# Moving the third sweep's last layer norm into both attention arms, with three carried tiles, and the last layer's pair products ahead of a weighing

## The chip, the cores and the metric

The kernel runs on one core of a Trainium2 chip as a single program. The metric is the device time in microseconds (us), as the median of several runs. A core has five engines, each with its own stream of instructions: PE (TensorE: matrix products and transposes; PEld is its weight load), DVE (VectorE), ACT (ScalarE), POOL (GpSimd) and SP (SyncE), which here issues most of the DMA transfers. The engines wait for each other through semaphores. SBUF is the memory that they compute from, PSUM holds PE's results in banks.

## The reference

Four graph layers act on x (4096 nodes by 64 features) with one dense 4096x4096 matrix `adj` of 64 MB, some 98% of it zero, symmetric in its pattern but not in its values. Each layer ends with a residual add and a layer norm.

```python
x = layernorm(x + cheb(x, adj, W0))        # K = 4: terms x, Lx, 2L(Lx)-x, ...; sum of terms @ W[k]
x = layernorm(x + attention_gru(x, adj, adj, ...))
x = layernorm(x + decay(x, adj, W2, b2))
x = layernorm(x + hyperbolic(x, adj, W3, b3))

# layer 1: A = adj without its diagonal d
node = concat([(A > 0) @ h, (A < 0) @ h]);  edge_out = gru_cell(node, h, ...)
hw = h @ W;  e_plus, e_minus = leaky_relu(concat of (A > 0) @ hw and (A < 0) @ hw, times a)
att = softmax(where(A > 0, e_plus, where(A < 0, e_minus, -9e15)), axis=1)
node_out = gru_cell((att * A) @ hw, h, ...)
out = d * edge_out + d * node_out

# layer 2: mask = adj != 0; rank = cumsum(mask, axis=1); k = min(deg, 100)
w = mask * 0.5 ** (k - pos);  out = w @ (x @ W2) + b2     # the last nonzeros of a row weigh most

# layer 3: logmap on the Poincare ball for every pair (i, j), weighted by adj / deg
out = expmap(0, (sum_j w_ij * logmap_xi(xj)) @ W3 + b3)
```

The data are never negative, but a negative entry of `adj` is allowed: the kernel counts negative row minima in the first sweep and chooses between two versions ("arms") of the attention at run time.

## The kernel before

`adj` is handled in tiles of 512 by 512 floats (1 MB): eight groups of 512 rows (`g`, NG = 8) by eight chunks of columns (`c`, NCH = 8), 64 tiles for one pass. A group is four blocks of 128 nodes (GB = 4). Features lie both as `nat_a` (nodes on partitions, 65 columns: 64 features and a one) and as `tr_a` (features on partitions), `sp_two` and `sp_lo` are its parts in narrower types for the attention's products.

**Chebyshev, 0 to 566 us.** A first sweep loads the 64 raw tiles, transposes them on PE and stores them as `adj_t`; a second and a third sweep read tiles of `adj_t` or keep raw ones in SBUF, in a rotating set of five 1 MB slots from the pools `staying` and `going`, handed out by `row_tile`. The third sweep (loop from L692) goes through the groups in the order 7, 0, 6, 1, 5, 2, 4, 3 (`last_row` is 3 in the changed code). When a group's products are done, steps from a list `due` follow: `third_weighed` (L655) weighs the sum with the last Chebyshev matrix, `after_third` (L659) transposes four blocks (L663), adds the residual on DVE (L665, "y"), runs the layer norm, centres `nat_a` (L301) and splits it into narrower types, and `turned_third` (L671) transposes the result back into `tr_a` (`to_columns`, L212). Ahead of the last group's steps, two tiles of attention's first row are loaded into slots (`with_at`) and one mask `adj > 0` is made of the first of them (`positives`, L447).

**Attention, to 865 us.** L1049 reads the flag from memory into a register of each engine, L1051 opens `If` (signed arm, both signs) and `Else` (unsigned arm). The code of the two arms lies one after the other in every engine's stream, so in the unsigned case each engine jumps over the signed arm at its start. Both arms come from `attention(signed, ...)`. It goes through 64 tiles; for each: a product of the mask with `sp_two` (L980, "wide"), one with `sp_lo` (L988, "narrow"), and one of the tile itself (after a step on DVE at L963) with `nat_a` (L997). The masks run two tiles ahead, and each is stored by a POOL DMA to `mask_t` (L724). In the last group, `load2` (L735 to L738) brings the masks of the decay's first chunk back from `mask_t` into eight SBUF tiles, `first_masks`. A group's tail (gates of two GRU cells, norm; `group_end`, L779 to L919) is cut into steps that run beside the next group's tiles; the end of it, `decay_parts`, prepares the next layer, its last operations being four POOL DMAs for each group. The arm ends with copies of `last_p` and `last_a` (L1040 to L1043).

**Decay, to 1067 us.** A tile's mask is counted from the end of the row by a product (L1192, `cnt_ps`), ACT or DVE makes the weight of it (L1197, L1199, `wt`), and PE gathers (L1150, L1162, `acc_ps`). Its sums are copied on DVE (L1215), weighed by PE (L1114, `wd`), and normed in steps. The steps of the last groups ("seam steps") are left over for the last layer.

**Last layer, from 1067 us.** For each group a "right" operand is made (L1283 to L1287); for each tile PE forms pair products `v_ps` (L1327), ACT squares them (L1336), DVE takes one off (L1353, `w`), ACT and DVE form the pair's factor through `rt` (L1545), `f` (L1530) and `at_d` (L1533), and PE gathers (L1387, L1392). Twelve small constants for it are made on DVE just ahead. One seam step, a weighing, is popped before the first rights and products.

Order: a tile scheduler puts the instructions of each engine into an order and gives each a slot in its pool; SP's DMA issues keep program order. An engine executes its own stream in order, so an instruction that waits holds those behind it.

Of the kernel before, what the change touches and what calls it, by code (L numbers as in the profile page):

```python
# [60 lines left out]
def gnn4_kernel(  # L61
# [25 lines left out]
    GB = 4  # L87
# [14 lines left out]

    front = ctx.enter_context(ExitStack())
    front_p = front.enter_context(tc.tile_pool(name="front", bufs=1, side="right"))

    staying_p = front.enter_context(tc.tile_pool(name="staying", bufs=2, side="right"))
    going = ctx.enter_context(ExitStack())
    going_p = going.enter_context(tc.tile_pool(name="going", bufs=3, side="right"))
    places = []

    def row_tile(name):
        places.append(name)
        pool = staying_p if len(places) % 5 in (1, 2) else going_p
        return pool.tile([P, GB, CB * P], F32, name=name, tag="raw")
# [63 lines left out]
    negatives = keep.tile([1, 1], mybir.dt.int32, name="negatives")  # L178
# [26 lines left out]
    def gblocks(g):  # L205
        return slice(g * GB, (g + 1) * GB)
# [238 lines left out]
    def positives(pool, at):  # L445
        pos = pool.tile([P, CB, GW], MASK, name="pos")
        in_order(nc.vector.tensor_scalar(pos, at, 0.0, None, ALU.is_gt, saturate=False))  # L447
        return pos

# [6 lines left out]
    with tc.tile_pool(name="acc", bufs=1) as acc_p, tc.tile_pool(name="win", bufs=1) as win_p, tc.tile_pool(  # L456
# [41 lines left out]

        def mine(g):
            return slice(g % 2 * F, g % 2 * F + F)  # L500
# [61 lines left out]

        loads, weight_steps = attention_weights(win_p, ps_p)
# [61 lines left out]
        for step in steps0:  # L625
            step()

# [6 lines left out]
        nc.vector.tensor_copy(negatives, low_ps)  # L634
# [20 lines left out]
        def third_weighed(g, ps):  # L655
            o, y_t = weigh(g, [(out_of(ps, "t_h"), cheb[:, 3, :])])
            nc.vector.tensor_tensor(y_t, o, y_t, ALU.add)

        def after_third(g):  # L659
            gs = gblocks(g)  # L660
            o = new_post()
            for b in range(GB):
                nc.tensor.transpose(o[:, b, :], acc_t[mine(g), g // 2, cols(b)], ident[mine(g), mine(g)])  # L663
            y = sm.tile([P, GB, F], F32, name="y0", tag="y")
            nc.vector.tensor_tensor(y, o, nat_a[:, gs, 0:F], ALU.add)  # L665
            layernorm(nat_a[:, gs, 0:F], y)
            centre(g)
            split(g, nat_a[:, gs, 0:F], F - 1, sp_hi, sp_mid, sp_lo)
# [23 lines left out]
        for m, g in enumerate(sum(([NG - 1 - i, i] for i in range(NG // 2)), [])):  # L692
            ps = ps_a.tile([P, GW], F32, name="pass3", tag=("h_ps", "w_ps")[m % 2])
            for c in reversed(range(g + 1)):
                at = load0(g, c)
                for k in range(CB):
                    halves(ps, 2, at[:, k, :], c * CB + k, c == g and k < 2, c == 0 and k >= CB - 2)
                later.flush()
                while due and due[0][0] <= n:
                    due.pop(0)[2]()  # L700
                n += 1
            due += [
                (n, m, lambda g=g, ps=ps: third_weighed(g, ps)), (n + 1, m, lambda g=g: after_third(g)),
                (n + 5, m, lambda g=g: turned_third(g)),
            ]
            due.sort(key=lambda d: d[:2])

        with_at = [load1(staying_p, NG - 1, c, "raw") for c in range(2)]
        with_pos = [positives(front_p, with_at[0])]
        for work in due:  # L710
            work[2]()

    going.close()
    three = ctx.enter_context(tc.tile_pool(name="three", bufs=1))

# [30 lines left out]
    first_masks = [late.tile([P, CB, GW], MASK, name=f"first_mask{n}") for n in range(2 * QG)]  # L746
# [6 lines left out]
    def group_end(g, Q, nb, tl, sums, a_t, wq, by_ln=False):  # L753
# [160 lines left out]
        def decay_parts(ps_p):  # L914

            split(g, nat_b[:, gblocks(g), :], F, sup_two[:, :, 0:F], sup_two[:, :, F : 2 * F], sup_lo)
            for there, here in ((over_two, sup_two), (over_lo, sup_lo)):
                for q in range(2):
                    nc.gpsimd.dma_start(  # L919
                        there[(1 - q) * HP : (2 - q) * HP, gblocks(g), :], here[q * HP : (q + 1) * HP, gblocks(g), :]  # L920
                    )
            nc.vector.tensor_tensor(
                nat_b[:, gblocks(g), :], nat_b[:, gblocks(g), :], bd.unsqueeze(1).to_broadcast([P, GB, F]), ALU.add
            )
# [13 lines left out]
        ] + norm, [[nothing]], [[decay_parts]]  # L938
# [5 lines left out]
    def attention(signed, cols_p, sg, tl, ps_a, ps_p):  # L944
# [68 lines left out]
        steps = []  # L1013
        for n, (g, c) in enumerate(order):
            if n + lead < len(order):
                ahead.append(masks(*order[n + lead]))
# [32 lines left out]
    any_negative = nc.values_load(negatives, min_val=0, max_val=P)  # L1049
    for signed in (True, False):  # L1050
        with tc.If(any_negative > 0) if signed else cmp.Else() as block:  # L1051
# [9 lines left out]

    nat_c = ctx.enter_context(tc.tile_pool(name="nat3", bufs=1, side="right")).tile([P, NB, F], F32, name="nat_c")
# [31 lines left out]
    def turn_prepared(ps_p, g):  # L1094
        to_columns(ps_p, tr_a[0 : F + 2, gcols(g)], left.pop(g), F + 2, nc.vector.tensor_copy)
        to_columns(ps_p, tr_o[0:2, gcols(g)], sides[:, gblocks(g), :], 2, nc.vector.tensor_copy)

# [39 lines left out]
    with tc.tile_pool(name="mask2", bufs=3) as mk_p, tc.tile_pool(name="wt2", bufs=3) as wt_p, tc.tile_pool(  # L1137
# [37 lines left out]
        for turn, groups in enumerate(turns_of):  # L1175
            cnt = [ps_c.tile([P, GW], F32, name=f"cnt_ps{a}") for a in range(2)]
            acc = [ps_a.tile([P, GW], F32, name=f"acc_ps{q}") for q in range(QG)]
            if turn == 0:
# [49 lines left out]
    middle.close()  # L1228

# [13 lines left out]
    with tc.tile_pool(name="o3", bufs=1) as op, tc.tile_pool(name="cols3", bufs=3) as cols_p, tc.tile_pool(  # L1243
# [4 lines left out]
        name="ps_p3", bufs=2, space=PSUM  # L1248
    ) as ps_p, tc.tile_pool(name="ps_a3", bufs=2, space=PSUM) as ps_a:
# [3 lines left out]

        to_right = op.tile([P, F + 2], F32, name="to_right")
        to_other = op.tile([P, 2], BF16, name="to_other")

        spread = op.tile([P, F + 1], F32, name="spread")
        spread_w = op.tile([P, F], F32, name="spread_w")
        wh_x = op.tile([P, F], F32, name="wh_x")
# [6 lines left out]

        nc.vector.memset(to_right, 0.0)
        nc.vector.tensor_scalar_mul(to_right[0:F, 0:F], ident[0:F, 0:F], -4.0)
        nc.vector.tensor_scalar_mul(to_right[F : F + 2, F : F + 1], ident[F : F + 2, F + 1 : F + 2], 2.0)
        nc.vector.tensor_scalar_mul(to_right[F : F + 2, F + 1 : F + 2], ident[F : F + 2, F : F + 1], 2.0)  # L1270
        nc.vector.memset(to_other, 0.0)
        nc.vector.tensor_scalar_mul(to_other[0:2, 0:1], ident[0:2, 1:2], OPPOSITE)
        nc.vector.tensor_scalar_mul(to_other[0:2, 1:2], ident[0:2, 0:1], OPPOSITE)
        nc.vector.memset(wh_x, 0.0)
        nc.vector.tensor_copy(wh_x[0:F, :], wh)
        nc.vector.tensor_copy(spread[:, 0 : F - 1], pair[:, 0 : F - 1])
        nc.vector.tensor_scalar(spread[:, F - 1 : F], pair[:, F - 1 : F], -1.0, None, ALU.add)
        nc.vector.tensor_copy(spread[:, F : F + 1], pair[:, F - 1 : F])
# [220 lines left out]
        if seam:  # L1499
            seam.pop(0)(ps_p)  # L1500
# [109 lines left out]
```

## Time and profile before

| what | value |
|---|---|
| runs of the kernel | 1541.69, 1551.27, 1553.98 us; median 1551.27 |
| profiled execution: time | 1546.41 us |
| profiled execution: span of the trace | 1544.3 us, 19446 instructions |
| PE busy | 1410.2 us (91%), 7054 instructions |
| DVE busy | 1066.9 us (69%), 2123 |
| ACT busy | 761.4 us (49%), 1265 |
| POOL busy | 123.8 us (8%), 194 |
| granted PE clock, mean | 0.977 |
| DMA | 385 MB, mean 250 GB/s |
| chain that ended last, by engine | PE 32%, DVE 18%, ACT 6%, issue 2%, DMA 2% |

Busy time is that of the whole span; the stages differ in what limits them, so a share says little about one of them. "Issue" in a chain is time in which an engine waited for nothing that the trace shows. In a line of the timeline the columns are: start (us), length (us), engine, line of the kernel and operation, output and inputs, shapes and types, and in brackets the idle time ahead of it on its engine with what ended it. An x4 or x16 joins so many like instructions. The engine names with a q stand for an engine's sequencer, where branches and register loads run.

### The profile page before, as it was taken

The page shows a single profiled execution, that of the slowest core. Times are in us where ns is not written, and L with a number is a line of the kernel's source. Part 1 is how long each engine was busy: PE and PEld are TensorE (multiplying, and loading weights), DVE is VectorE, ACT ScalarE, POOL GpSimd, SP SyncE. Part 2 cuts the span into 40 slices and gives each one's busy share as a digit, 9 for nine tenths or more (in the row PEclk, how much of TensorE's full clock was granted, in tenths as well). Part 3 has the DMA queues.
Part 4 walks back from the last instruction along what each step waited for, and adds up shares of the span by engine and source line. Part 5 has one row for each costly group of instructions (what it writes and reads, how often), then busy time and mean ns, then how long its engine had stood idle before and what let it go on. Part 6 is the DMA issues. An engine that isn't in the chain of part 4 may idle for free.

```text
span 1544.3 us, 19446 instructions
## 1 busy us (share of the span) xinstructions
PE 1410.2 (91%) x7054; PEld 644.7 (42%) x7054; DVE 1066.9 (69%) x2123; ACT 761.4 (49%) x1265; POOL 123.8 (8%) x194
## 2 busy tenths in 40 slices
PE   5999999999999969889899999998888999899995
PEld 4555655554443323334343333333334444344343
DVE  5899989883000663667666422556999999999997
ACT  3544434441000110222222476654877999899995
POOL 3011000000000001222222200000000000000000
PEclk9999999999999998999999999999999999999997
DMA  9999999996787987888888655553224453445430
GB/s 295 412 404 411 411 410 397 382 358 242 245 287 261 389 342 271 280 309 305 296 309 296 207 177 183 164 165 131 88 109 164 162 195 136 167 156 193 149 113 11
DMA packets 103359, 385.38 MB, mean 250 GB/s; under 512 B 16340, under 2 KB 17368, under 8 KB 71256
## 3 DMA queue, kind: packets, MB, share of 16 engines
q1 hardware_dynamic: 84256, 296.78, 53.9%
q0 software_dynamic: 15616, 85.73, 13.6%
q10 hardware_dynamic: 3384, 1.56, 0.4%
q8 instruction: 57, 0.93, 0.2%
q14 instruction: 46, 0.38, 0.1%
HBM read 297.26 MB, written 85.20 MB: 248 GB/s over the span
## 4 chain that ended last, share of the span: by engine, by line
PE 32%; DVE 18%; ACT 6%; issue 2%; DMA 2%; SPq 0%; ACTq 0%; DVEq 0%
PE v_ps L1327 5%; PE a_ps L997 4%; PE sums_ps L1387 4%; PE cnt_ps L1192 4%; PE acc_ps L1150 4%; DVE rt L1545 3%; DVE at_m L1373 3%; PE p_ps L980 2%; DVE f L1530 2%; DVE at_d L1533 2%; ACT wt L1197 2%; PE post L779 1%; DMA at<-adj_t 1%; PE p_ps L988 1%; DVE w L1353 1%
## 5 line engine op out<-in xcount | busy, mean ns | idle before, releaser
L592 ACT COPY at<-tp 128x512 f32<-128x512 f32 x256 | 132.5, 598 | 137.2 <-issue 96.0
L1327 PE MATMUL v_ps<-rv,tr_a 128*128 128x512 f32 (+1 forms) x288 | 141.5, 616 | 31.7 <-DVE rt L1545 30.3
L1197 ACT ACTIVATE wt<-cnt_ps 128x512 uint16<-128x512 f32 x208 | 115.4, 594 | 72.1 <-PE cnt_ps L1192 70.3
L585 PE MATMUL tp<-ident,raw 128*128 128x128 f32 x1024 | 133.4, 284 | 16.2 <-DMA raw<-in_adj_dram 12.0
L618 DVE TENSOR_REDUCE dpart<-raw 128x4 f32<-128x2048 f32 x64 | 145.4, 2272 | 0.4 <-DMA raw<-in_adj_dram 0.3
L620 DVE TENSOR_REDUCE lows<-raw 128x1 f32<-128x2048 f32 x64 | 145.4, 2271 | 0.0
L1387 PE MATMUL sums_ps<-at_d,nat_c 128*64 128x512 f32 x288 | 139.8, 606 | 1.4 <-DVE at_d L1533 1.0
L585 PEld LDWEIGHTS tp<-ident,raw 128*128 128x128 f32 x1024 | 116.6, 145 | 55.3 <-issue 34.1
L997 PE MATMUL a_ps<-at,nat_a 128*64 128x512 f32 x512 | 126.9, 624 | 2.9 <-DVE at L963 2.9
L447 DVE TENSOR_SCALAR pos<-at 128x2048 fp8e4<-128x2048 f32 x72 | 87.1, 1224 | 58.1 <-DMA at<-adj_t 49.3
L1392 PE MATMUL sums_ps<-at_m,nat_c 128*64 128x512 f32 x224 | 108.6, 607 | 0.0
L492 PE MATMUL w_ps<-at,cheb_n 128*128 128x512 f32 x224 | 101.1, 595 | 0.0
L492 PE MATMUL pass<-at,cheb_n 128*128 128x512 f32 x224 | 99.9, 604 | 0.7 <-DVE cheb_n L643 0.7
L1556 ACT ACTIVATE rt<-rt,one_col 128x1024 f32<-128x1024 f32 x72 | 78.7, 1095 | 22.5 <-DVE rt L1545 22.0
L1327 PEld LDWEIGHTS v_ps<-rv,tr_a 128*128 128x128 f32 x288 | 52.8, 199 | 82.7 <-DVE rt L1545 39.5
L1545 DVE SCALAR_TENSOR_TENSOR rt<-v_ps,rt 128x1024 f32<-128x1024 f32 x72 | 83.2, 1156 | 3.8 <-ACT rt L1521 3.6
L1192 PE MATMUL cnt_ps<-m,follow 128*64 128x512 fp8e4 x480 | 81.1, 391 | 4.7 <-ACT wt L1197 2.3
L1533 DVE TENSOR_TENSOR at_d<-at_d,f 128x1024 f32<-128x1024 f32 x72 | 83.2, 1156 | 0.1
L1530 DVE SCALAR_TENSOR_TENSOR f<-rt,w 128x1024 f32<-128x1024 f32 x72 | 82.9, 1158 | 0.5 <-ACT rt L1556 0.4
L1373 DVE TENSOR_TENSOR at_m<-post,at_m 128x512 f32<-128x512 f32 x112 | 75.3, 683 | 9.3 <-PE post L1371 8.6
L1336 ACT ACTIVATE w<-v_ps,one_col 128x1024 f32<-128x1024 f32 x72 | 75.7, 1053 | 11.3 <-PE v_ps L1327 10.9
L1547 ACT ACTIVATE w<-w,half_shift 128x1024 f32<-128x1024 f32 x72 | 78.7, 1094 | 0.9
(365 smaller groups left out, 2267.3 us busy)
## 6 DMA issues: line engine op xcount, KB each, us to landing
at<-adj_t SPq DMA_DIRECT2D x122, 1024.0 KB, 6.1
raw<-in_adj_dram SPq DMA_DIRECT2D x64, 1024.0 KB, 13.7
adj_t<-at POOLq DMA_DIRECT2D x64, 1024.0 KB, 8.2
at_d<-adj_t SPq DMA_DIRECT2D x36, 1024.0 KB, 4.8
at_m<-adj_t SPq DMA_DIRECT2D x28, 1024.0 KB, 6.8
mask_t<-pos POOLq DMA_DIRECT2D x64, 256.0 KB, 5.9
m<-mask_t SPq DMA_DIRECT2D x120, 128.0 KB, 2.8
m<-mask_t SPq DMA_DIRECT2D x60, 256.0 KB, 3.9
```

The source lines that it names most:

```text
L492: in_order(nc.tensor.matmul(ps, lhsT=cheb_n[:, jb, k : k + 2, :], rhs=rhs, start=first, stop=last))
L585: in_order(nc.tensor.transpose(tp[:, cols(b)], raw[:, b, cols(k)], ident))
L592: nc.scalar.copy(at[:, k, :], tp)
L618: in_order(nc.vector.tensor_reduce(dpart[:, g, c, :], raw, AX.X, ALU.add))
L620: in_order(nc.vector.tensor_reduce(lows[:, n : n + 1], raw.rearrange("p b j -> p (b j)"), AX.X, ALU.min))
L997: in_order(nc.tensor.matmul(ps[q * F : (q + 1) * F, :], lhsT=nat_a[:, c * CB + k, 0:F], rhs=parts[q if signed else 0][:, k, :], start=(c = ...
L1192: in_order(nc.tensor.matmul(cnt[a][r * HP : (r + 1) * HP, :], lhsT=follow, rhs=chunks[c][odd][2 * a + r][:, k, :], start=(h == 2 * NB - 1) ...
L1197: in_order(nc.scalar.activation(wt[odd][a], cnt[a], AF.Relu, scale=-128.0))
L1327: nc.tensor.matmul(vs[n][:, k, cs], lhsT=tr_a[:, cols(jb)], rhs=rights[i][0][:, cs], start=True, stop=True)
L1373: work.append(lambda to=to, tp=tp: nc.vector.tensor_tensor(to, tp, to, ALU.mult))
L1387: in_order(nc.tensor.matmul(bank[0:F, :], lhsT=nat_c[:, j * CB + k, :], rhs=own[t][:, k, :], start=(i == j and k == 0), stop=(j == seq[-1] ...
L1545: nc.vector.scalar_tensor_tensor(rt, vs[n][:, :, cs], V_FLOOR, rt, ALU.max, ALU.add)
```

## The change

In the third sweep the last group (3) is only weighed, into a tile of its own, `sum_last`. Its norm, now the function `normed_third`, runs inside the attention, at the first tile of either arm; the transposes back to `tr_a` become the fourth of the steps that run beside the first tiles. The five slots of `row_tile` come from other pools in the order going, going, staying, staying, front. Three tiles instead of two are carried into the attention, with three masks made ahead of the branch. The flag is turned round (`no_negative`), so that the unsigned arm comes first in the code and the signed arm is the `Else`. The eight `first_masks` lie in the memory of two of the carried tiles. The POOL DMAs of `decay_parts` get a step of their own. The last layer's constants are built in the second turn of the decay (`constants3`), in memory of attention constants that are no longer needed; its PSUM pools change places, and the seam step that stood ahead of its first rights and products is no longer popped there, so each later one follows one iteration later. In the stream as built, the constants stand at decay's start on DVE.

```diff
+    staying_p = staying.enter_context(tc.tile_pool(name="staying", bufs=2, side="right"))
     front_p = front.enter_context(tc.tile_pool(name="front", bufs=1, side="right"))
-    staying_p = front.enter_context(tc.tile_pool(name="staying", bufs=2, side="right"))
-    going_p = going.enter_context(tc.tile_pool(name="going", bufs=3, side="right"))
+    going_p = going.enter_context(tc.tile_pool(name="going", bufs=2))
+    five = (going_p, going_p, staying_p, staying_p, front_p)
     def row_tile(name):
         places.append(name)
-        pool = staying_p if len(places) % 5 in (1, 2) else going_p
+        return five[(len(places) - 1) % 5].tile([P, GB, CB * P], F32, name=name, tag="raw")
...
+    def normed_third(g, y_t, ps_p):
+        gs = gblocks(g)
+        o = ps_p.tile([P, GB, F], F32, name="post", tag="post")
+        for b in range(GB):
+            nc.tensor.transpose(o[:, b, :], y_t[:, cols(b)], ident[mine(g), mine(g)])
+        y = sm.tile([P, GB, F], F32, name="y0", tag="y")
+        nc.vector.tensor_tensor(y, o, nat_a[:, gs, 0:F], ALU.add)
+        layernorm(nat_a[:, gs, 0:F], y)
+        centre(g)
+        split(g, nat_a[:, gs, 0:F], F - 1, sp_hi, sp_mid, sp_lo)
...
-        nc.vector.tensor_copy(negatives, low_ps)
+        nc.vector.tensor_scalar(no_negative, low_ps, 0.5, None, ALU.is_lt)
...
         def third_weighed(g, ps):
-            nc.vector.tensor_tensor(y_t, o, y_t, ALU.add)
+            nc.vector.tensor_tensor(sum_last[mine(g), :] if g == last_row else y_t, o, y_t, ALU.add)
...
+            due.append((n, m, lambda g=g, ps=ps: third_weighed(g, ps)))
+            if g != last_row:
+                due += [(n + 1, m, lambda g=g: after_third(g)), (n + 5, m, lambda g=g: turned_third(g))]
-        with_at = [load1(staying_p, NG - 1, c, "raw") for c in range(2)]
-        with_pos = [positives(front_p, with_at[0])]
+        with_at = [load1(pool, NG - 1, c, "raw") for c, pool in enumerate((staying_p, staying_p, front_p))]
+        with_pos = [positives(ahead_p, at, bufs=3) for at in with_at[:1]]
         for work in due:
             work[2]()
+        with_pos += [positives(ahead_p, at, bufs=3) for at in with_at[1:]]
...
-    first_masks = [late.tile([P, CB, GW], MASK, name=f"first_mask{n}") for n in range(2 * QG)]
+    first_masks = [
+        at.rearrange("p k i -> p (k i)").bitcast(MASK)[:, n * CB * GW : (n + 1) * CB * GW].rearrange(
+            "p (k i) -> p k i", k=CB
+        )
+        for at in with_at[:2] for n in range(QG)
+    ]
...
-        steps = []
+        steps = [nothing, nothing, nothing, lambda ps_p: to_columns(
+            ps_p, tr_a[0 : F + 1, gcols(last_row)], nat_a[:, gblocks(last_row), :], F + 1, nc.scalar.copy
+        )]
         for n, (g, c) in enumerate(order):
+            if n == 0:
+                normed_third(last_row, sum_last[mine(last_row), :], ps_p)
...
-    any_negative = nc.values_load(negatives, min_val=0, max_val=P)
-    for signed in (True, False):
-        with tc.If(any_negative > 0) if signed else cmp.Else() as block:
+    all_positive = nc.values_load(no_negative, min_val=0, max_val=1)
+    for signed in (False, True):
+        with cmp.Else() if signed else tc.If(all_positive > 0) as block:
...
+    def constants3():
+        to_right = const.tile([P, F + 2], F32, name="to_right", tag="wih_pp")
+        to_other = const.tile([P, 2], BF16, name="to_other", tag="wih_mm")
+        spread = const.tile([P, F + 1], F32, name="spread", tag="whh_e")
+        wh_x = const.tile([P, F], F32, name="wh_x", tag="whh_n")
+        nc.vector.memset(to_right, 0.0)
+        nc.vector.tensor_scalar_mul(to_right[0:F, 0:F], ident[0:F, 0:F], -4.0)
...
+            if turn:
+                to_right, to_other, spread, wh_x = constants3()
...
     ) as rp, tc.tile_pool(name="ps_v3", bufs=2, space=PSUM) as ps_v, tc.tile_pool(
-        name="ps_p3", bufs=2, space=PSUM
-    ) as ps_p, tc.tile_pool(name="ps_a3", bufs=2, space=PSUM) as ps_a:
+        name="ps_a3", bufs=2, space=PSUM
+    ) as ps_a, tc.tile_pool(name="ps_p3", bufs=2, space=PSUM) as ps_p:
...
-        if seam:
-            seam.pop(0)(ps_p)
         rights[seq[0]] = right(seq[0])
         product(0)
         square(0)
```

## The prediction

> **What bounds the kernel now.** I read the table of stages first, cut at the two seams that the change touches; columns are stage, its length, then busy microseconds (and instructions) of PE, PEld, DVE, ACT and POOL, the granted PE clock, the DMA share and GB/s.
>
> ```profile
> 566.00:582.00 16.00, 3.71 (x16) 1.88 (x17) 8.78 (x30) 1.96 (x4) 2.26 (x3) 0.73 1.00 392
> 582.00:865.00 283.00, 262.10 (x1248) 108.98 (x1247) 177.65 (x510) 58.40 (x121) 68.85 (x92) 0.97 0.80 287
> 865.00:1067.00 202.00, 196.33 (x1638) 70.00 (x1639) 80.42 (x273) 123.78 (x235) 3.44 (x5) 1.00 0.52 158
> 1067.00:1082.00 15.00, 8.85 (x35) 4.03 (x31) 12.79 (x64) 7.01 (x13) 2.43 (x5) 0.88 0.91 365
> 1200.00:1300.00 100.00, 93.10 (x393) 41.33 (x389) 97.97 (x145) 94.85 (x125) 0.00 (x0) 1.00 0.45 171
> ```
>
> Attention (582 to 865) and decay (865 to 1067) are PE's: it is busy 93% and 97%. The last layer is DVE's, with ACT and PE close behind. PE is nearly empty in two places: seam A, 566 to 582, and seam C, 1067 to 1082. The timeline of seam A, PE and DVE:
>
> ```profile
> 568.60 0.46 PE L663 MATMUL post<-ident,acc_t 64*128 64x64 f32 x4 [0.20 <-DVE acc_t L657]
> 575.00 1.09 PE L212 MATMUL post<-ident,nat_a 128*65 128x128 f32 x4 [5.94 <-DVE nat_a L301]
> 581.50 1.89 PE L980 MATMUL p_ps<-pos,sp_two 128*128 128x512 fp8e4 x4 [5.41 <-issue]
> 582.95 0.36 DVE L1007 TENSOR_TENSOR wq<-wq_signed 128x192 f32<-128x192 f32 x1 [6.20 <-issue]
> ```
>
> PE waits 5.94 us for the last norm on DVE, then 5.41 us for "issue". The view of line 1051, where each engine chooses its arm, names the second wait (durations in ns, then the start):
>
> ```profile
> L1051 SPq COMPARE_BRANCH  x1: 50/50/50, 566.4 to 566.4; - x1
> L1051 PEldq COMPARE_BRANCH  x1: 5825/5825/5825, 575.6 to 575.6; - x1
> L1051 ACTq COMPARE_BRANCH  x1: 54/54/54, 576.7 to 576.7; - x1
> L1051 DVEq COMPARE_BRANCH  x1: 72/72/72, 577.1 to 577.1; - x1
> ```
>
> All of them jump over the signed arm here. SP goes on at once (75 rows to skip); PE (2,673 rows) stands for 5.8 us, and DVE, whose record is short, executes nothing until 582.95, 5.8 us after its branch. Code packets follow the three long jumps: 16 KB at 578.9, 8 KB at 579.9 and 580.6. Reading the flag costs about 0.5 us (475 to 545 ns).
>
> **Part 1, seam A.** Before: the last sweep product ends at 566.0, the first attention product starts at 581.5, and the fourth tile's at 593.6 (the three tiles between take 12.1 us, partly at half clock). Now only the weighing of the last row and three masks stand ahead of the branch, and the unsigned arm is the one that falls through.
> - Loads: the three carried tiles take the oldest of the five slots, which come free as the sweep's tiles end (556.8, 560.3, 562.4); the two of before were issued at 564.3 and 566.0. The DMA queues were idle from 560 to 565. They land by about 567.5, 4.8 us after issue.
> - DVE: the add ends at 568.54; three masks at 1.23 us end at 572.3; flag and branch 0.45 us, wq 0.36 us; the norm's y starts at 573.1. By the trace of before y to the centred nat_a takes 4.46 us and to sp_lo 6.36 us: 577.6 and 579.5. A fourth mask ends at 580.7.
> - PE: its flag and branch lie beside the transposes before (568.39). The moved four transposes run at 568.6 as now, the first attention product when mask 0 is there, 569.85. A tile costs 0.97 + 0.55 + 1.72 = 3.24 us at full clock, and the first three need nothing of row 3, so the fourth starts at 579.6. It wants nat_a (577.6), then a mask 1.7 us later (580.7, in time).
> That is 593.6 - 579.6 = 14.0 us. A tile moves 1 MB in and 0.25 MB of mask out, 3.1 us at the seam's 400 GB/s, hardly less than PE's 3.24, and the loads start only 7 us sooner: I take 1.2 us off, so -12.8.
>
> The unknown is a branch that is not taken: no row shows one. From above 5.8 us as on PE, from below the 0.05 us of SP's row. I take 0.05, because what follows is the code that comes next anyway. At 5.8 PE would start at 574.1, DVE would have nat_a at 583.0 and the fourth mask at 586.1, three cold tiles would end at 586.2: -7.4.
>
> **Part 2, the jump comes back at seam B.** At the arm's end every engine must now skip the signed arm. Before, the end of the arm lay next to the decay code:
>
> ```profile
> 864.73 0.59 ACT L1043 COPY last_a<-a_ps 128x512 f32<-128x512 f32 x1 [1.29 <-PE a_ps L997]
> 865.86 0.60 ACT L1197 ACTIVATE wt<-cnt_ps 128x512 uint16<-128x512 f32 x1 [0.55 <-PE cnt_ps L1192]
> 865.37 0.62 PE L1192 MATMUL cnt_ps<-first_mask,follow 128*64 128x512 fp8e4 x4 [0.68 <-ACT last_a L1043]
> ```
>
> The seam costs 0.7 us now. [...] So a far jump is paid at B by PE, DVE and ACT. DVE's last work ends at 860.8, so it is back in time (about 866.5). PE can dispatch its last products ahead, as it did at 575.0, so some is hidden. ACT cannot: it reaches the jump with the copy of last_a at 864.75, and behind it stand the weights (wt) that PE needs from its second count on. With 5.8 us ACT is back at 870.5, 4.6 late. At A the queues were saturated (DMA share 1.00), at B they are half so; the fetch may take about 4.4 us, an estimate between 0.05 and 5.8 nearer the row: 3.3 late. PE, idle that long, comes back at half clock (the tiles after the 5.41 wait lost 2.4 us): 1.8. Its 0.6 us wait at 880.8 for the mask load disappears. B = +4.5, bounds 0 and +7.
>
> **Part 3, seam C.** Chain and timeline of before (PE, ACT, DVE's first rt):
>
> ```profile
> 1069.77 2.00 PE L1114 MATMUL post<-wd,sums 128*128 128x64 f32 x16 [2.36 <-DVE sums L1215]
> 1074.16 3.08 PE L1327 MATMUL v_ps<-rv,tr_a 128*128 128x512 f32 x7 [0.20 <-ACT rv L1284]
> 1081.26 1.82 DVE L1545 SCALAR_TENSOR_TENSOR rt<-v_ps,rt 128x1024 f32<-128x1024 f32 x2
> 1082.54 6.77 PE L1327 MATMUL v_ps<-rv,tr_a 128*128 128x512 f32 x8 [3.79 <-DVE rt L1545]
> ```
>
> In the order as built, "right" now follows the last gather directly (its bank is one that the copies of sums do not hold), then six of the eight weighings, then the pair products. From 1067.24: right 1.25 us, six weighings (12 passes of 0.115) to 2.7 us, v_ps at 1069.9 instead of 1074.16; ACT's squares about 4.8 us sooner. But DVE is the bound here. Out of its way go twelve constants (1069.68 to 1070.96, 1.3 us), now in decay, where DVE is 40% busy. Against it: its next instructions are the two w, which wait for those squares, 3.1 us of new idle time with y and all of the norm queued behind, where it had 2.2 us of idle time before; and some 5.5 us of norm work moves behind the first rt. DVE idles 2.4 us in 1082 to 1120 and 9 us to 1200, which the earlier start can fill. Bounds -4.8 (all of the start) and +1; I take -2, nearer DVE's account.
>
> **Small edits.** The copies of the decay parts get a step of their own, in the same order on POOL: 0. Mask loads now fill the carried tiles; on SP two or three tile loads go ahead of each, which waited behind it (29.6 us in four waits on mask_t). PE's gaps beside them (1.08 us at 694.7 and 729.3) are as long where no such wait stands (803.0, 837.7): 0, at best -1. The constants in decay wait for the last gates (877.1) ahead of one gate read; two weights go from DVE to ACT at 0.60 us: +0.3 together.
>
> Sum: -12.8 + 4.5 - 2 + 0.3 = -10.0 us against the profiled execution (span 1544.3, with what lies around it 1546.4): 1536.4. The median of the runs is 1551.27, 4.9 above it; carried over, 1541.
>
> **Rivals.** *The far jump is hidden* ([...]PE and ACT reach it early) and C keeps its start: -12.8 + 1 - 4.5 = -16.3, 1535. For it SP's 50 ns, against it the three code packets. *A branch stalls even when not taken*: -7.4 + 4.5 - 2 = -5, 1546. *Seam C turns against it, slower*: with the norm steps behind stage work, PE waits at the next pair products for DVE as at 1082.54, where 3.8 us of waiting cost another 3.4 at half clock, 7.2 together; one more such stall plus a full DVE idle of 3.1 and +1 for crowding is +11.3, total -12.8 + 4.5 + 0.3 + 11.3 = +3, 1554. It decides once C costs over 8 us. Against it: the starts of PE and ACT move earlier, and DVE's total work falls.
>
> **Numbers.** Forecast 0.6 (1535 to 1548), hidden jump 0.2, not-taken stall 0.1, seam C 0.1. The range 1530 to 1552 leaves out most of seam C's case and the far end of the hidden jump. The runs lie 0.8% apart, so about 1% is what a measurement can tell from no change, 15.5 us: the hidden jump and a little of the forecast reach it. Faster 0.22, same 0.73, slower 0.05.
>
> **What would show it.** The branch record on PE in the new trace near 568 with some 50 ns, the first attention product near 570 and the fourth tile's near 580; DVE's y near 573; a long record of the unconditional branch on PE at the arm's end, code packets there, and ACT's first wt 3 to 5 us after last_a; v_ps 2.7 us after the last gather, and rt 4 to 5 us sooner. Wrong would be: a not-taken branch of microseconds, DMA waits of masks before the fifth tile, or no gap at B.

## The result, and the profile after

The changed kernel takes 1536.75 us (median of 13 runs, 1530.06 to 1539.54), the kernel before in the runs beside it 1548.62 us (13 runs, 1541.69 to 1553.98). The ratio is 0.9915, 95% interval 0.9898 to 0.9932: 0.85% faster, a little inside the 1% that was named as the bound. 1541 was forecast, range 1530 to 1552. The profiled execution's span is 1535.0 us, 9.3 below that of before; a second profile of each (E11, E12) gives 22.0, so one pair of profiles doesn't measure the gain.

The table of stages of the kernel after is cut at its own seams: last sweep product to first attention product, attention to its last product, decay to its last gather, and from there to the first rt. Columns are those of the table before.

```profile
564.28:568.14 3.86, 2.10 (x12) 1.02 (x12) 2.99 (x6) 1.17 (x2) 1.17 (x1) 1.00 0.58 219
568.14:852.06 283.92, 262.88 (x1252) 110.51 (x1251) 183.83 (x535) 59.13 (x122) 70.39 (x95) 0.97 0.83 298
852.06:1058.72 206.66, 198.73 (x1641) 70.96 (x1642) 80.20 (x284) 124.88 (x237) 3.75 (x5) 0.99 0.51 155
1058.72:1068.52 9.80, 6.84 (x31) 3.89 (x31) 5.83 (x25) 5.64 (x8) 2.43 (x5) 1.00 0.88 345
```

By the same cuts of the trace before: the third sweep ends 1.7 us earlier (in the 14 profiles here it ends anywhere from 564.0 to 567.8, so that isn't the change), attention including its start is 287.8 instead of 298.7 us (-10.9), the decay 206.7 instead of 202.7 (+3.9), the last layer to the end of the span 476.3 instead of 476.9 (-0.6). That is -9.3.

**Seam A.** The timeline of the kernel after, PE and DVE:

```profile
567.40 0.43 PE L463 MATMUL post<-ident,sum_last 64*128 64x64 f32 x4 [0.72 <-ACT tr_a L214]
568.14 1.02 PE L1004 MATMUL p_ps<-pos,sp_two 128*128 128x512 fp8e4 x4 [0.31 <-DVE pos L448]
571.20 0.43 DVE L465 TENSOR_TENSOR y<-post,nat_a 128x256 f32<-128x256 f32 x1
```

Both long waits of before (5.94 us for the norm, 5.41 us of "issue") are gone. The fourth tile starts 13.2 us after the last sweep product instead of 27.5. But the gain does not last: the thirteenth tile starts 55.4 us after it instead of 64.8. In between PE waits once more. The timeline of DVE and PE there:

```profile
601.80 1.23 DVE L448 TENSOR_SCALAR pos<-at 128x2048 fp8e4<-128x2048 f32 x1 [4.29 <-DMA at<-adj_t]
603.76 1.62 PE L895 MATMUL post<-wq,a_t 128*128 128x192 f32 x4 [3.10 <-DVE n L821]
```

and the table of stages around it, where the granted clock (the share of full speed at which PE was let run; 1 is full) falls to 0.51 behind the wait:

```profile
600.00:605.00 5.00, 1.90 (x8) 1.46 (x6) 3.13 (x15) 0.93 (x3) 0.54 (x1) 0.81 0.99 395
605.00:610.00 5.00, 5.00 (x15) 1.27 (x14) 2.61 (x10) 1.10 (x4) 0.54 (x1) 0.51 0.86 328
```

DVE waits for a tile, and SP's own waits say why that tile came late (560 to 640 us; total, times, longest):

```profile
SPq L752 <- DMA mask_t<-pos: 9.5, 1, 9.5
```

SP stood 9.5 us, until 595.99, at the load of the first of `first_masks`, which needs a mask's store. The three tile loads queued behind it went out one after the other from 596.6. The scheduler had moved that load up, to some seven tile loads behind the branch.

**Seam B.** The branch of the kernel after has two records on each engine, at the arm's start and end (min/median/max in ns, first and last start):

```profile
L1079 PEldq COMPARE_BRANCH  x2: 92/2024/3957, 565.7 to 848.1; - x2
L1079 ACTq COMPARE_BRANCH  x2: 38/46/53, 567.3 to 852.1; - x2
```

Behind the second one the timeline of ACT and PE shows:

```profile
852.10 0.59 ACT L1071 COPY last_a<-a_ps 128x512 f32<-128x512 f32 x1 [1.29 <-PE a_ps L1021]
852.74 0.59 PE L1242 MATMUL cnt_ps<-at,follow 128*64 128x512 fp8e4 x3 [0.68 <-ACT last_a L1071]
855.11 0.60 ACT L1247 ACTIVATE wt<-cnt_ps 128x512 uint16<-128x512 f32 x1 [2.42 <-issue]
855.23 1.88 PE L1242 MATMUL cnt_ps<-at,follow 128*64 128x512 fp8e4 x5 [1.90 <-issue]
```

The branch that isn't taken costs PE 92 ns. The jump at the arm's end costs PE 3.96 us, all hidden: PE dispatched it at 848.1, and its last product ended at 852.06. Then two stops show: ACT's (2.42 us), and a second one of PE after three counts (1.90 us). The trace's code packets go with both stops of PE. One of 16 KB ends at 850.65, and the branch record 1.43 us later; the next runs from 852.83 to 853.85, and PE goes on 1.37 us later. The first weight starts 3.05 us after the last product instead of 1.18, the first gather 8.9 instead of 5.4.

**Seam C.** Timeline, first products and rt of the last layer:

```profile
1061.83 2.80 PE L1359 MATMUL v_ps<-rv,tr_a 128*128 128x512 f32 x8
1068.52 1.22 DVE L1575 SCALAR_TENSOR_TENSOR rt<-v_ps,rt 128x1024 f32<-128x1024 f32 x1
1069.80 5.40 PE L1359 MATMUL v_ps<-rv,tr_a 128*128 128x512 f32 x8 [3.83 <-DVE rt L1575]
```

The first rt comes 9.8 us after the last gather instead of 13.8; the next products wait 3.8 us for it as before. Some of the lead goes to the norm's steps behind it, as PE's next long wait shows, of before and then of after:

```profile
1093.90 1.98 PE L1327 MATMUL v_ps<-rv,tr_a 128*128 128x512 f32 x4 [2.25 <-DVE rt L1545]
```

```profile
1081.81 3.75 PE L1359 MATMUL v_ps<-rv,tr_a 128*128 128x512 f32 x4 [4.82 <-DVE rt L1575]
```

It is longer, and half clock follows it (0.50 from 1081.8 to 1086.8). The third rt's lead is 3.5 us, and from the sixteenth rt to about the fortieth the lead is a steady 1.4 us.

### The profile page after: what moved, and what is told of

Its sections match the earlier page's. It is cut to its first block, busy times and chain, and to the rows that moved or that the text cites. A ratio compares the mean times of both kernels' runs of the same rounds, so it can differ in the third digit from the quotient of the medians.

```text
span 1535.0 us, 19444 instructions
## 1 busy us (share of the span) xinstructions
PE 1408.3 (92%) x7054; PEld 645.1 (42%) x7054; DVE 1064.4 (69%) x2121; ACT 762.8 (50%) x1267; POOL 124.4 (8%) x194
## 3 DMA queue, kind: packets, MB, share of 16 engines
q1 hardware_dynamic: 84256, 296.78, 54.1%
## 4 chain that ended last, share of the span: by engine, by line
PE 65%; DVE 20%; ACT 7%; DMA 5%; issue 3%; SPq 0%; ACTq 0%; POOL 0%; DVEq 0%; POOLq 0%
PE tp L604 7%; PE pass L512 6%; PE w_ps L512 6%; PE v_ps L1359 5%; PE sums_ps L1419 4%; PE a_ps L1021 4%; PE cnt_ps L1242 4%; PE acc_ps L1198 4%; PE pass L505 4%; PE h_ps L505 4%; DVE at_m L1405 3%; DVE rt L1575 3%; PE p_ps L1004 2%; PE post L523 2%; ACT wt L1247 2%
## 5 line engine op out<-in xcount | busy, mean ns | idle before, releaser
L1359 PE MATMUL v_ps<-rv,tr_a 128*128 128x512 f32 (+1 forms) x288 | 138.4, 604 | 33.6 <-DVE rt L1575 29.9
L1419 PE MATMUL sums_ps<-at_d,nat_c 128*64 128x512 f32 x288 | 143.2, 619 | 1.4 <-DVE at_d L1563 1.0
```

The costliest lines, as they stand in the source:

```text
L1359: nc.tensor.matmul(vs[n][:, k, cs], lhsT=tr_a[:, cols(jb)], rhs=rights[i][0][:, cs], start=True, stop=True)
L1419: in_order(nc.tensor.matmul(bank[0:F, :], lhsT=nat_c[:, j * CB + k, :], rhs=own[t][:, k, :], start=(i == j and k == 0), stop=(j == seq[-1] ...
```

## The experiments

All are edits of the changed kernel, except E1 (an edit of the kernel before) and the second profiles E11 and E12. Of each profile the table gives, in us: the start of the fourth and of the thirteenth tile after the last sweep product, attention from the last sweep product to its last product, the decay from there to its last gather, and the rest of the span. The ratio is to the kernel before, runs of the same chip, with its 95% interval. A tile starts with the first of its 16 products. The expectations call the thirteenth the twelfth, having twelve ahead of it, and read both times more roughly, from merged rows of the timeline: for the changed kernel 12.9 (in E2 14.9) and 54.5, for the one before 27.6.

| kernel | ratio of times | 4th | 13th | attention | decay | last layer |
|---|---|---|---|---|---|---|
| before | 1 | 27.5 | 64.8 | 298.7 | 202.7 | 476.9 |
| before, second profile (E12) | | 28.5 | 65.4 | 302.9 | 202.7 | 479.7 |
| after | 0.9915 (0.9898 to 0.9932) | 13.2 | 55.4 | 287.8 | 206.7 | 476.3 |
| after, second profile (E11) | | 13.2 | 54.1 | 282.2 | 208.1 | 473.8 |
| E1 arms swapped alone | 0.9944 (0.9923 to 0.9965) | 21.2 | 58.4 | 292.3 | 205.8 | 478.8 |
| E2 signed arm first | 0.9881 (0.9849 to 0.9913) | 17.7 | 55.6 | 287.5 | 203.2 | 476.1 |
| E3 no signed arm | 0.9889 (0.9860 to 0.9917) | 13.2 | 56.2 | 290.3 | 203.2 | 473.5 |
| E4 copies behind the branch | 0.9903 (0.9882 to 0.9925) | 13.2 | 58.5 | 290.4 | 206.4 | 473.6 |
| E5 first masks late | 0.9877 (0.9859 to 0.9895) | 13.2 | 52.0 | 281.2 | 207.8 | 473.9 |
| E6 E4 and shifted target | 0.9896 (0.9876 to 0.9916) | 13.2 | 53.1 | 281.6 | 202.9 | 472.4 |
| E7 E5 and E6 | 0.9847 (0.9830 to 0.9864) | 13.2 | 50.9 | 277.3 | 202.9 | 475.9 |
| E8 seam C undone | 0.9927 (0.9902 to 0.9952) | 13.2 | 53.2 | 280.9 | 208.1 | 479.1 |
| E9 norm ahead of the branch | 0.9928 (0.9900 to 0.9957) | 19.9 | 56.7 | 290.7 | 206.5 | 474.0 |
| E10 two tiles, one mask | 0.9897 (0.9862 to 0.9931) | 16.3 | 53.8 | 287.5 | 207.0 | 476.4 |

The attention of after, its second profile and E8 is the same code: 287.8, 282.2 and 280.9 us, at granted clocks of 0.970, 0.988 and 0.994. Length times clock is 279 in all three, so a difference of up to 7 us in that column is the clock of an execution. For the two profiles of before the same product is 286.7 and 287.5 (298.7 x 0.960, 302.9 x 0.949): some 8 us of the gain in attention don't come from the clock, an estimate.

**A second profile of each kernel** (E11, E12):

> The changed kernel itself, for a second profile. If the attention stage's 287 us at a granted clock of 0.97 in the first profile were that execution's own: last sweep product to last attention product between 280 and 290 us, with the granted clock going the other way; the order of waits, the 3 to 4 us at the ninth tile and the stop after the jump at the same places.

> The kernel before itself, for a second profile: the 5.9 us wait for the norm and the 5.4 us behind the branch at seam A and 0.7 us at seam B at the same places with the same length; the stage lengths differ from the first profile by a few us with the granted clock.

The waits are where they were: for before 6.64 us for the norm (0.7 longer), 5.54 behind the branch, 0.68 at seam B; for after 2.59 us at the tenth tile (0.5 shorter), 2.06 behind the jump. The spans are 1550.2 and 1528.2 us. What differs most is how PE comes back from a wait. In the last layer both kernels have a wait of 2.21 us at the fortieth rt. The timeline of PE there, of before, of after and then of after's second profile:

```profile
1323.75 3.30 PE L1327 MATMUL v_ps<-rv,tr_a 128*128 128x512 f32 x4 [2.21 <-DVE rt L1545]
```

```profile
1313.68 3.78 PE L1359 MATMUL v_ps<-rv,tr_a 128*128 128x512 f32 x4 [2.21 <-DVE rt L1575]
```

```profile
1308.38 1.98 PE L1359 MATMUL v_ps<-rv,tr_a 128*128 128x512 f32 x4 [2.21 <-DVE rt L1575]
```

Four equal products after an equal wait: 3.30 us, 3.78, and 1.98. The granted clock is 0.50 to 0.52 from 1313 to 1319 in the first profile of after, and 1.00 at that place in the second. In the first PE stayed slow for three more pairs, and exactly there the lead of 1.4 us was lost; in the second the end of the layer came 2.5 us earlier. So the same wait in the same kernel can be followed by half clock or by none; what decides it these rows don't show.

**E1: arms swapped in the kernel before.**

```diff
-        nc.vector.tensor_copy(negatives, low_ps)
+        nc.vector.tensor_scalar(negatives, low_ps, 0.5, None, ALU.is_lt)
...
-    for signed in (True, False):
-        with tc.If(any_negative > 0) if signed else cmp.Else() as block:
+    for signed in (False, True):
+        with cmp.Else() if signed else tc.If(any_negative > 0) as block:
```

> The kernel before with one edit: the flag turned round and the unsigned arm put first; norm, carried tiles, seam C as before. Jump theory (a far taken jump costs where it is taken): at seam A the 5.4 us of idle time behind PE's branch go, the wait for the norm (5.9 us) stays, so last sweep product to fourth tile falls from 27.6 to about 21.5 us; at seam B the decay stage (last attention product to last gather) grows from 202.6 to about 206.4 us. Sum -2 us, ratio to before about 0.9985. Rival (the longer decay stage of the changed kernel comes from its mask loads and constants, not from the jump): decay stays at 202.6, sum -6 us, ratio 0.996.

The 5.4 us at A went, the wait for the norm stayed (6.17 us): fourth tile -6.3, thirteenth -6.4. The decay grew by 3.1 us. So the swap alone brings the jump to B. Its time fell by 0.56%, 8.7 us of 1551, more than the 2 us expected; its stages show 3.3 of it (-6.4 + 3.1), and the profile is of the slowest of its six runs. The rest stays open.

**E2: signed arm first again.**

```diff
-        nc.vector.tensor_scalar(no_negative, low_ps, 0.5, None, ALU.is_lt)
+        nc.vector.tensor_copy(no_negative, low_ps)
...
-    for signed in (False, True):
-        with cmp.Else() if signed else tc.If(all_positive > 0) as block:
+    for signed in (True, False):
+        with tc.If(all_positive > 0) if signed else cmp.Else() as block:
```

> The changed kernel with one edit: the signed arm first again, so that the jump is taken at seam A; norm in the arms, three tiles and masks, seam C as changed. Jump theory: PE stands 4 to 5.8 us at its branch and comes back at half clock, so last sweep product to fourth tile grows from 14.9 to about 20.5 us; the decay stage falls from 206.4 to 202.6. Sum about +2 us on the changed kernel, some 1538. Rival (the jump at A would now lie beside the masks and the norm on DVE, and cost little): A stays within 2 us of 14.9, and the kernel is 2 to 4 us faster than the changed one.

PE's branch record is 3.3 us at A, and PE comes back late and at about half its pace, 1.89 us for four products that take 1.02 in the changed kernel (timeline of this run):

```profile
571.31 0.66 PE L463 MATMUL post<-ident,sum_last 64*128 64x64 f32 x4 [2.66 <-issue]
571.90 1.89 PE L1004 MATMUL p_ps<-pos,sp_two 128*128 128x512 fp8e4 x4
```

The fourth tile is 4.5 us later than in the changed kernel, as the jump theory has it. But PE waits only 1.79 us at the tenth, where the changed kernel waits 3.10 and 2.59, and the thirteenth starts at 55.6 us, 0.2 to 2.4 later than in the three profiles of the changed attention (55.4, 54.1, 53.2). The decay is 203.2, shorter by 3.5 and 4.9. So most of the jump is hidden at A without the swap, and paid at B with it. Neither theory held whole: the fourth tile is the jump theory's, the total nearer the rival's. The time points the same way (0.9881 against 0.9915), but the intervals overlap, so that E2 is faster isn't shown.

**E3: no signed arm.** The version for a negative matrix is left out, the branch stays.

```diff
-    for signed in (False, True):
+    for signed in (False,):
```

> The changed kernel without the signed arm (the version for a matrix with negative entries is left out; the branch itself stays), so nothing lies behind the unsigned arm to jump over. Jump theory: last_a to the first weight falls from 3.0 to about 1.1 us, the decay stage from 206.4 to 202.6, sum -4 us, some 1533. Rival (mask loads and constants make the decay stage longer): decay stays at 206, the time at 1537.

PE's record at the arm's end is 0.18 us. First weight 1.18 us after the last product, first gather 5.44, decay 203.2, time 1533.37: the far jump is 3.5 us of the first profile's decay (4.9 of the second's), and the mask loads and constants add 0.4.

**E4: the last copies behind the branch.**

```diff
+    banks = [hold_p.tile([P, GW], F32, name=f"bank{n}") for n in range(4)]
...
-                nc.scalar.copy(w_t[0], wide_ps[0])
+                if g:
+                    nc.scalar.copy(w_t[0], wide_ps[0])
...
+    nc.scalar.copy(last_p[0], banks[2])
+    nc.scalar.copy(last_a, banks[3])
```

> The changed kernel with both arms, but the last two copies (last_p, last_a) stand behind the branch's end instead of in the arms: attention's PSUM banks are taken outside the arms, so that ACT takes its jump some 8 us before the last product ends. If ACT carries the cost of the jump: last product to first weight falls from 3.0 to about 1.0 us, the decay stage from 206.4 to about 202.5, sum -4 us, some 1533. If PE's own jump (a record of 3.96 us) carries it, or the loads: the decay stage stays above 205 us, the time at 1536 to 1537.

A half success. ACT takes its jump at 844.3, eleven us ahead of need, and its first weight is back at 1.18 us. The first gather still comes at 8.95, as PE's second stop stays (timeline of this run):

```profile
855.88 0.41 PE L1250 MATMUL cnt_ps<-at,follow 128*64 128x512 fp8e4 x2 [0.68 <-ACT last_a L1093]
857.97 0.62 PE L1250 MATMUL cnt_ps<-at,follow 128*64 128x512 fp8e4 x4 [1.68 <-issue]
```

PE and ACT were equally late; to mend one changes nothing. In E1 and E9, whose code differs, PE runs four counts and then waits 2.08 and 2.49 us for ACT's weight: there ACT's lateness is the one that shows.

**E6: E4, and PE's target shifted.**

```diff
-                normed_third(last_row, sum_last[mine(last_row), :], ps_p)
+                normed_third(last_row, sum_last[mine(last_row), :], ps_p, 10 if signed else 0)
...
-        for b in range(GB):
+        for b in [n % GB for n in range(GB + more)]:
```

> The kernel with the last two copies behind the branch, and ten more transposes in the signed arm, which doesn't run: they only shift the place that PE jumps to. Theory of the second block: PE ran two counts there and then stood 1.7 us because its code's next block had still to come; the shift puts the target early in a block, so that stop is gone, last product to first gather falls from 8.95 to about 5.5 us, the decay stage from 206.4 to about 203, sum -3.5 us. Rival (PE's stop has another cause, a load or a bank): decay stays at 206.

Ten transposes that never run took the stop away (timeline of this run):

```profile
849.64 0.62 PE L1250 MATMUL cnt_ps<-at,follow 128*64 128x512 fp8e4 x4 [0.68 <-ACT last_a L1093]
850.78 0.72 PE L1250 MATMUL cnt_ps<-at,follow 128*64 128x512 fp8e4 x4 [0.52 <-ACT wt L1255]
```

First gather 5.44, decay 202.9. There are still two 16 KB packets, at 846.0 and 849.2; only PE has no such stop beside the second, just the 0.52 us in which it waits for ACT's weight. The traces show what the stop goes with: in the six profiles that have it (after twice, E4, E5, E8, E10) PE goes on 1.37 to 1.45 us after the second packet's end, also in E5, where the row names a mask load. That the ten instructions moved the target so that this packet's code is needed later fits, but was not shown: which instructions a packet holds was not seen.

**E5: first masks late.**

```diff
     def load1(pool, g, c, tag="at", order=lambda ins: ins):
-        nc.sync.dma_start(at, adj_t[g][:, c * CB : (c + 1) * CB, :])
+        order(nc.sync.dma_start(at, adj_t[g][:, c * CB : (c + 1) * CB, :]))
...
-                at, pos = load1(cols_p, g, c), None
+                at, pos = load1(cols_p, g, c, order=in_order), None
...
-                load2(first_masks, turns_of[0], NCH - 1)
+                load2(first_masks, turns_of[0], NCH - 1, in_order)
```

> The changed kernel with one edit: the loads of the first masks (first_masks) keep their place of the program on SP, in the last group, instead of standing nine loads behind the branch. Queue theory: SP waits 9.5 us there for a mask's store, all tile loads behind it come late, DVE waits 4.3 us and PE 3.1 us for them, and PE goes on at half clock; without it the twelfth tile starts about 49.5 us after the last sweep product instead of 54.5, sum -5 us, some 1532. Rival (the tile loads are limited by the DMA queues' rate there, share 0.9 to 1.0, whatever stands on SP): the twelfth tile stays at 53 us or later, the time at 1536 to 1537.

`in_order` keeps an instruction's place in the program, here that of the tile loads of the attention too. SP's wait on a mask's store is gone, and PE's wait at the tenth tile is 0.96 us, where after, its second profile, E3, E4, E6 and E8 had 2.2 to 5.2. The thirteenth tile starts at 52.0 us against 53.1 to 58.5 in those. The time is 1530.05 us, 0.4% below the changed kernel with intervals just apart: the queue theory held in its wait and its sum. The thirteenth tile shows 1.2 to 3.4 us of it against the same code without the edit (after twice, E8), and attention as a whole none (281.2 against 280.9 in E8); where the rest lies was not found.

**E7: all three edits.**

> All three edits in one: copies behind the branch, shifted target of PE's jump, first masks loaded late. If the gains add up: twelfth tile at about 49.5 us, decay stage about 203, some 8 us below the changed kernel, 1528 to 1529. If the earlier tiles are only given back at a later wait: 1532 to 1533.

1524.66 us (5 runs, 1524.31 to 1527.99), ratio 0.9847: 1.5% below before, and 0.7% below the changed kernel (0.9847 / 0.9915 = 0.993). Against E6, which lacks only the late masks, it is 0.5% faster, with intervals apart. It is the fastest kernel of the case, and leaves nothing out that the changed one computes.

**E8: seam C undone.**

```diff
-        name="ps_a3", bufs=2, space=PSUM
-    ) as ps_a, tc.tile_pool(name="ps_p3", bufs=2, space=PSUM) as ps_p:
+        name="ps_p3", bufs=2, space=PSUM
+    ) as ps_p, tc.tile_pool(name="ps_a3", bufs=2, space=PSUM) as ps_a:
...
+        if seam:
+            seam.pop(0)(ps_p)
```

> The changed kernel with the last layer's two edits undone: PSUM pools in the old order and the weighing popped ahead of the rights; the constants stay in the decay. Theory of a kept lead (DVE sets the pace of the layer, a lead of 1.4 us at its first rt's lasts to the end; only one execution's half clock hid it): last gather to first rt 12.5 us or more instead of 9.8, last gather to the end of the span 1.4 to 2.5 us longer, some 1538 to 1539. Rival (the lead is given back inside the layer): first rt as late, but the end within 0.5 us of the changed kernel.

First rt at 15.5 us, last layer 479.1; the ten profiles with the new seam have 472.4 to 476.4, mean 474.6; the four with the old one 476.9 to 479.7. So seam C brought some 4.5 us in the profiles (479.1 - 474.6). The medians can't tell it (0.9927 against 0.9915). The lead is kept; that it looked spent in the first profile was the clock at the fortieth rt.

**E9 and E10: parts of seam A,** the norm ahead of the branch first, then two tiles and one mask.

```diff
-            if g != last_row:
-                due += [
+            due += [
...
-            if n == 0:
-                normed_third(last_row, sum_last[mine(last_row), :], ps_p)
...
```

> The changed kernel with the last norm and its transposes back ahead of the branch, as before; three tiles and masks, order of arms, seam C as changed. If the norm inside the arms carries the gain: PE waits some 6 us for it again, the first attention product starts about 10 us after the last sweep product instead of 3.9, the fourth tile at about 19 us instead of 12.9, and the kernel loses 3 to 6 us, some 1541. If the wait for the first mask load on SP pins the ninth to twelfth tile anyway: the twelfth tile stays at 52 to 55 us and the time within 2 us of the changed kernel.

```diff
-        with_at = [load1(pool, NG - 1, c, "raw") for c, pool in enumerate((staying_p, staying_p, front_p))]
+        with_at = [load1(pool, NG - 1, c, "raw") for c, pool in enumerate((staying_p, staying_p))]
...
-        with_pos += [positives(ahead_p, at, bufs=3) for at in with_at[1:]]
```

> The changed kernel with two carried tiles and one mask ahead of the branch instead of three and three; the norm stays in the arms. If tiles and masks are what the norm hides behind: PE has one tile's work and then waits for masks that stand behind the norm or beside it on DVE, the fourth tile starts 4 us or more later than 12.9 us, and the time rises by 2 to 5 us, to 1539 to 1542. If the norm alone carries it: the fourth tile within 1.5 us, the time the same.

With the norm ahead of the branch PE waits 5.38 us again, and the fourth tile is 6.7 us later; with two tiles and one mask PE waits 2.38 us at the third, and the fourth is 3.1 us later. But at the tenth tile they wait 1.08 and 0.96 us instead of 2.6 to 3.3, so part of it comes back: the thirteenth is at 56.7 and 53.8 us, against 53.2 to 55.4 in the changed attention. The times lie within its interval. Beside SP's mask load, neither part is worth anything by itself that these runs can measure; the norm's may be 1.3 to 3.5 us by the thirteenth tile.

## Why the prediction was right

The time lies in the range and on the right side; the chance for "within 1%" was 0.73, and 0.85% came. The sum was -10.0; the medians lie 11.9 apart, the ratio of the runs makes -13.2 (0.0085 x 1549). Of the 4.3 us between the forecast of 1541 and the median, 2.7 are the kernel before itself: 1551.27 in its first three runs, 1548.62 in thirteen. That the sum fits is partly luck: seam A gave less than was booked, seam C more by about as much.

- **The branch not taken.** 0.05 was taken from SP's row, between 0.05 and 5.8 us. PE's record is 0.092. Right, and the rival with a stall there fell.
- **Seam A up to the fourth tile.** Right, step by step. -14.0 was worked out, -14.3 measured (13.2 - 27.5), -15.3 between the second profiles. After the last sweep product the first attention product came at 3.86 us (3.85 worked out), y at 6.9 (7.1), the fourth tile at 13.2 (13.6).
- **Seam A as a whole.** Two terms were too small. The discount for slower loads was set at 1.2 us, from 3.1 us for the transfers of a tile; with 1024 KB in and 256 KB out at its 400 GB/s (392 in its table) it is 3.28, no faster than PE's 3.24. (The queues before the seam were idle from 562.1, not 560: their share is 0.64 and 0.16 in the two us from 560.) And the mask loads on SP were put at "0, at best -1", because two or three tile loads were said to go ahead of each. Measured, that step is a wait of 9.5 us with the tile loads behind it, 3.1 us of idle PE and half clock; E5 takes it away. By the thirteenth tile the gain is 9.4 us (11.3 between the second profiles), not 12.8. The prediction looked at the waits on mask stores of before and found PE unhurt there; it didn't ask what an earlier PE would find in that queue.
- **Seam B.** +4.5 forecast, +3.9 and +5.4 measured, 3.5 and 4.9 shown by E3 to be the jump. That the far jump is paid at all was the author's estimate, drawn from PE's row of 5.8 us against SP's of 50 ns, and it held: PE's record at B is 3.96 us and ends 1.43 us after a code packet. ACT was named as the carrier: it was late by 1.9 us, but PE's second stop was as late, which the prediction did not have. E4 shows that ACT was not the only carrier, E6 that both together are. The half clock after the stop came as forecast (L801's pair takes 1.24 us, in before 0.71; the granted clock is 0.50 from 857 to 859).
- **The swap's worth.** The prediction booked the jump's removal as part of -12.8 at A and +4.5 at B, and took it for a gain. In the kernel before it is one (E1). E2 shows that with norm, tiles and masks moved most of the jump at A is hidden by the thirteenth tile (0.2 to 2.4 us are left), so that the swap costs its 3.5 to 4.9 us at B for less than that. This is the largest error of reasoning behind a right number.
- **Seam C.** PE was not "nearly empty" there: it is busy for 8.85 of the 15 us. First rt "4 to 5 us sooner", 4.0 measured. -2 was chosen between -4.8 and +1; the profiles say about -4 (mean 474.6 against 478.6 of before twice, E1 and E8). So the term was undersized by 2 us, although DVE's idle time to 1200 that was to be filled is 7.0 us (2.4 + 4.6), not 9. The rival that turned it into a loss fell: the wait at the next products is 3.83 us as before (3.79), and there is not one stall more. But two of the later ones are longer, 4.82 us at the fourth rt and 3.74 at the twelfth, where before had 2.25 at the third and 2.56 at the fourteenth. Across the first of them the lead falls from 5.4 us at the fourth rt to 0.7 at the sixth.
- **The hidden jump** as a rival (1535) is nearer the median than the forecast, but it was not what happened: the jump shows at B in both profiles of the changed kernel.

Open: how much of attention's later part (thirteenth tile to end: 233.9 and 237.5 us before, 232.4, 228.1 and 227.8 after) belongs to the change, since the granted clock moves it by as much.

## What to carry to other kernels

A gain at the head of a stage is worth only what the next limit lets through (here 14.3 us at the fourth tile, 9.4 at the thirteenth): follow it for ten tiles, through the queue that feeds them, and look there for an instruction that waits for a store. A jump over code that is not run had its price where it was taken (3.3 to 5.9 us in PE's branch record), so leave it where another wait covers it, or let each engine reach it early, and look behind its target for a second stop, which a shift of the code can remove (1.68 us in E4, gone in E6). When two engines come back equally late, only an edit to both shows (decay 206.4 us with ACT's lateness alone mended, 202.9 with both).

## What the runs showed of the hardware

A far taken jump held PE for 3.3 to 4.0 us in these runs (3.33 in E2, 3.42 in E6, 3.96 in the changed kernel), and for 5.8 and 5.9 us in the two profiles of before. In all thirteen such records the end comes 1.3 to 1.6 us after the end of a 16 KB code packet (1.55 in before, 1.43 in after); what differs is when that packet starts, 0.9 to 1.6 us after the branch, and 3.4 in both profiles of before. The prediction put the length down to full DMA queues. That alone it isn't: the share was 1.00 there, but E2's jump at A, with 0.89 over the 5 us around it, took 3.3 us, and the changed kernel's at B, with 0.36 from 848.1 to 852.1, took 3.96. ACT goes on late too, by 2.2 to 2.5 us of idle time, though its branch record is 0.04 us.

PE could then stop a second time for 1.5 to 2.1 us after two or three products, again until 1.4 us after a 16 KB code packet. Ten instructions in code that is not executed removed that stop (1.68 us in E4, none in E6).

The same wait of 2.21 us on PE was followed by half clock for some 6 us in one execution of the changed kernel (0.51 from 1313 to 1319) and by none in another (1.00). Such differences move a stage of 280 us by up to 7, while its length times the granted clock stays the same.
